# Which queue sends the first unit's stacks, and 4 passes of zeros ahead of its scores, not 18

## The chip, the core and the metric

The kernel runs on one core of a Trainium2 chip. The metric is the device time of one execution in microseconds (us), the median over the runs. A core has TensorE (PE: matmuls, with weight loads listed apart as PEld), VectorE (DVE), ScalarE (ACT), GpSimd (POOL) and SyncE (SP), and 16 DMA engines. A transfer is issued by an instruction on SP, ACT or POOL; the issuing instruction takes time on that engine's queue, and the transfer itself then runs on the DMA engines. Engines wait for each other, and for transfers, by semaphores.

## What is computed

One transformer block on x (16 batch entries of 256 tokens, 256 wide), with a conditioning vector and a context per batch entry:

```python
shift_a, scale_a, gate_a, shift_m, scale_m, gate_m = jnp.split(silu(c) @ W_mod + b_mod, 6, axis=-1)
x_norm = modulate(_ln(x), shift_a, scale_a)
q, k, v = jnp.split(x_norm @ W_qkv + b_qkv, 3, axis=-1)          # 16 heads of 16
attn_w = softmax(einsum('bhqd,bhkd->bhqk', q, k) * scale)
x = x + gate_a * (einsum('bhqk,bhkd->bhqd', attn_w, v) @ W_proj + b_proj)
...
x = x + cross_attention(_ln(x), _ln(context))
...
x = x + gate_m * (gelu(modulate(_ln(x), shift_m, scale_m) @ W_mlp1 + b_mlp1) @ W_mlp2 + b_mlp2)
```

All of it is float32. Matmuls of precision that matters are done as sums of products of a high part and a low remainder (the names with h_ or Th and l_ or Tl).

## The kernel before, in words

The work is cut into 32 units: for each batch entry one of self-attention ("s") and one of cross-attention ("c"); the MLP follows behind them. A unit needs its queries and keys in a *stack*: big[n % 3], a tile with one half for q and one for k, in which every head's rows hold the high part twice and the low part once, so that one matmul gives the precise product. A stack half is written by six transfers of 128 KB (out of h_q or h_k: words x0, x1, y0, y1; out of l_q or l_k: words l0, l1), for two column halves f = 0, 1. The function that issues one is `send` in `to_stack`; it takes the queue as an argument. Before the rows are sent, the tile is set to zero (words z0q, z0k and so on), since rows that are not sent must be zero.

The ramp, before the first unit can run, is written out by hand: the string PRE in the table E_ (line 55) lists words, and each word issues its instructions in that order. All engines keep this order in the program. The words that matter here:

- K0a, K0m: the key matmuls of unit 0 into ps_k; K0h: ScalarE reads them into h_k; K0l: VectorE makes the remainder l_k. Q0a, Q0m, Q0h, Q0l the same for queries; K1..., Q1... for unit 1.
- K0x0, K0x1, K0y0, K0y1, K0l0, K0l1 and the same with Q: the twelve sends of unit 0's stack. A word without a suffix goes on SyncE; with p, on GpSimd.
- hiv, lov: high part and remainder of V's weights (ScalarE, VectorE); V0a, V0b: the value matmuls of unit 0 (psv_s); bv: a bias product into st, added by VectorE into bqkv.
- b9: `busy(9, sp[0])`, nine matmuls of a 128 x 128 tile of zeros (wz) with itself. Each is two passes on TensorE, so the trace counts 18. Their result is not read.
- L2a, L2b, L2c: layer norm of unit 2 (VectorE's statistics, GpSimd's power and apply, xn_s), which TensorE transposes (psT_s) soon after the first scores.
- ld3: the load of x for unit 3, on SyncE.

Behind PRE, the loop over units begins with n = -1: eight beats, in which the scores of unit 0 (s_tile: q from big times k from big, into st or s) are computed and VectorE takes their row maxima (mx). These first scores are the first readers of unit 0's stack.

Transfers on the hardware queues (SP and ACT) take eight semaphores in turn, DMAHW0 to DMAHW7, and a transfer isn't issued before the one that had its semaphore last has landed. GpSimd's have semaphores of their own (DMASW).

Of the kernel before, what the change touches and what calls it, by code (L numbers as in the profile page):

```python
# [21 lines left out]
def pixart_block(  # L22
# [29 lines left out]
                return tc.keep_in_program_order(i) if self.on else i  # L52
            return issue

    E_ = {'M': (-10, -4, 1, 5), 'CUT': 8, 'LN': {'s': 'pool', 'c': 'pool', 'q': 'pool'}, 'ON': (1, 1, 1), 'L0': -16, 'L1': 1, 'S0': -7, 'A0': 0, 'T0': 1, 'S1': 5, 'A1': 7, 'L2': 9, 'T1': 9, 'S2': 32, 'AP': 23, 'DV': (0, 1), 'HP': (1, 0), 'BZ': {}, 'AV': {1: [(1, 2), (1, 3)], 9: [(0, 0), (0, 1)]}, 'AHEAD': (0, 0, 0, 0, 0, 2), 'TW': {(21, 6): 'cb', (23, 6): 'u1', (25, 1): 'u0', (25, 7): 'u2', (27, 1): 'u3', (27, 4): 'h2p', (27, 5): 'h3p', (28, 3): 'u5 h1p', (28, 4): 'h0p', (29, 0): 'l3', (29, 1): 'l0', (29, 3): 'l1d', (29, 6): 'u7', (29, 7): 'u4 u6 h4p', (30, 1): 'h5p h6d', (30, 7): 'l6', (31, 0): 'h7p', (31, 1): 'l4', (31, 2): 'l5', (31, 6): 'l7', (28, 1): 'l2'}, 'XP': 1, 'IL': 1, 'MF': 0, 'SH': 4, 'RAMP': 1, 'HA': 1, 'MP': 16, 'W': (7, 1, 0, 0), 'PRE': 'z0qp z0kp load rest ld2 one0 silu b12 brow L0a turn L0b b4 L0d scale T0t sc1 hik lok L1a T0h L1b T0l b4 shift hiq K0a L1d bk loq K0m K0h K0x0 K0x1 K0y0p K0y1p T1t K0l T1h K0l0 K0l1 bq T1l Q0a Q0m Q0h Q0x0 Q0y0p Q0x1 Q0y1p Q0l Q0l0 Q0l1 z1kp z1qp K1a K1b hiv lov Q1a Q1b K1x0 K1x1 K1y0 K1y1 K1l K1l0 K1l1 Q1x0 Q1x1 Q1y0 Q1y1 Q1l Q1l0 Q1l1 L2a L2b L2c V0a V0b bv b9 ld3', 'SL': {(-1, 0): 'V1a', (-1, 1): 'T2t T2h T2p vone z2kp z2qp', (-1, 2): 'V1b', (-1, 3): 'rest wm', (-1, 4): 'M0 rest one1 ld4', (-1, 5): 'K2a L3a', (-1, 6): 'K2m L3b L3p L3c', (-1, 7): 'mods sc2 one2 rest', (0, 0): 'gm rest', (0, 1): 'rest', (0, 4): 'rest', (0, 6): 'rest', (1, 0): 'rest', (1, 5): 'rest'}}

    PE = InOrder(nc.tensor, True)
    ACT, DVE, POOL, SP = (InOrder(e, True) for e in (nc.scalar, nc.vector, nc.gpsimd, nc.sync))
# [49 lines left out]
    brow = const.tile([32, P], F32, name="brow")  # L108
# [8 lines left out]
    def split(hi, lo, src, eng=POOL, hp=0):  # L117
        (DVE, POOL, ACT)[E_['HP'][hp]].tensor_copy(hi, src) if E_['HP'][hp] < 2 else ACT.copy(hi, src)
        eng.tensor_tensor(lo, src, hi, ALU.subtract)
# [9 lines left out]
    sc1 = const.tile([P, 2, 2, B], F32, name="sc1")  # L129
    bT = const.tile([P, 32], F32, name="bT")  # L130
    sT = const.tile([P, KC, B], F32, name="sT")
    cb = const.tile([P, H], F32, name="cb")
# [123 lines left out]
    wm = []  # L256
# [9 lines left out]
    gm = []  # L266
# [19 lines left out]
    def layernorm(src, name):  # L286
# [19 lines left out]

        def apply(eng=E_['LN'].get(name[0])):
            o.xn = work.tile([P, NT, H], F32, tag="xn", name=f"xn_{name}", bufs=3)
            if eng == "act":
                nb = work.tile([P, NT], F32, tag="nb", name=f"nb_{name}")  # L310
                DVE.scalar_tensor_tensor(nb, o.mv[:, :, 0], -1.0, o.rs, ALU.mult, ALU.mult)
            if eng not in ("act", "dve"):
                less = work.tile([P, NT], F32, tag="less", name=f"less_{name}")
                POOL.tensor_scalar(less, o.mv[:, :, 0], -1.0, None, ALU.mult)
            for t in range(NT):
                if eng == "act":
                    ACT.activation(o.xn[:, t], src()[:, t], AF.Identity, bias=nb[:, t:t + 1],
                                   scale=o.rs[:, t:t + 1])
                elif eng == "dve":
                    DVE.tensor_scalar(o.xn[:, t], src()[:, t], o.mv[:, t, 0:1], o.rs[:, t:t + 1],  # L320
                                      ALU.subtract, ALU.mult)
                else:
                    POOL.tensor_scalar(o.xn[:, t], src()[:, t], less[:, t:t + 1], o.rs[:, t:t + 1],
                                       ALU.add, ALU.mult)
# [476 lines left out]
    M = {}  # L801
# [52 lines left out]
    def mlp_T(b):  # L854
# [18 lines left out]
        for f in range(KC):  # L873
            DVE.tensor_scalar(y[:, f], pst[:, f * N:(f + 1) * N], sc1[:, 1, f, b:b + 1],
                              cpT[:, 6 + f, b:b + 1], ALU.mult, ALU.add)
        if b in E_['DV']:
            DVE.tensor_copy(hi, y)
# [111 lines left out]
    rest = setup_rest()  # L989

    u0, u1 = units[:2]
# [4 lines left out]
    u2 = units[2]  # L996
    word = {}
    for n, v in (("0", u0), ("1", u1), ("2", u2)):
        for c in "KQV":
            o = getattr(v, c)  # L1000
# [8 lines left out]
    for n, v in (("0", u0), ("1", u1), ("2", u2)):  # L1009
        word["T" + n + "t"], word["T" + n + "h"], word["T" + n + "l"] = v.T[0].parts  # L1010
        word["T" + n + "p"] = v.T[0].low_pool
        for c in "KQ":
            o = getattr(v, c)
            word[c + n + "l"] = o.parts[2]
            word[c + n + "m"], word[c + n + "h"] = o.third, o.high
            word[c + n + "p"] = o.low_pool
            for f in range(KC):
                for q, k in enumerate("xyl"):
                    word[f"{c}{n}{k}{f}"] = lambda o=o, q=q, f=f: o.send(f, q)
                    word[f"{c}{n}{k}{f}p"] = lambda o=o, q=q, f=f: o.send(f, q, POOL)  # L1020
            word[c + n + "s"] = lambda o=o: [o.send(f, q) for f in range(KC) for q in range(3)]
    for n in range(2):
        for i in range(16):
# [15 lines left out]
    u3 = units[3]  # L1039
# [9 lines left out]
    for i in range(3):  # L1049
        for n, f in (("b", f_b), ("hi", f_hi), ("lo", f_lo)):  # L1050
            word[n + "qkv"[i]] = lambda f=f, i=i: f(i)
    for w in E_['PRE'].split():
        word[w]()
    for p, ws in E_['SL'].items():
        at[p] += [word[w] for w in ws.split()]
    ACT.on, POOL.on, SP.on = E_['ON']
    at_end = defaultdict(list)
# [172 lines left out]
    last, o, q = units[-1], units[-1].post, units[-2].post  # L1230
# [115 lines left out]
```

## Time and profile before

| | before |
|---|---|
| median of 3 runs | 735.78 us (735.75 to 736.23) |
| the profiled execution | 736.51 us, of which the span 734.7 us |
| PE / DVE / ACT / POOL busy | 99% / 77% / 77% / 71% of the span |
| granted TensorE clock | 0.999 of full speed |

The span is what the trace covers; the time of the same execution is 1.8 us longer. TensorE is busy nearly all of it. The chain of waits, followed back from the end, has this share by engine:

```profile
PE 90%; POOL 2%; DVE 2%; issue 2%; ACT 2%; DMA 1%; SPq 1%; ACTq 0%; POOLq 0%; DVEq 0%
```

A row of the timeline has the start in us, the length in us, the engine, the line of the code (L51 for nearly all, where a helper records the operations), the operation, the tile written and the tiles read with their shapes, and a count when like rows are merged; in brackets, the idle time just before it and what ended it. SPq, ACTq and POOL with DMA_DIRECT2D are the issues of transfers. Rows of a table by windows have the window, its length, the busy time of PE, PEld, DVE, ACT and POOL, the granted clock, the share of the DMA engines and GB/s.

GpSimd's four issues, which the change takes from it:

```profile
13.94 1.31 POOL L51 DMA_DIRECT2D big<-h_k  x2 [1.56 <-ACT h_k L51]
16.66 1.05 POOL L51 DMA_DIRECT2D big<-h_q  x2 [1.42 <-ACT h_q L51]
```

### The profile page before, as it was taken

How to read it: one execution, taken by the hardware profiler on the slowest of the kernel's cores; microseconds unless marked ns; L12 is line 12 of the kernel's file. 1: busy time of each engine (PE TensorE's matmuls, PEld its weight loads, DVE VectorE, ACT ScalarE, POOL GpSimd, SP SyncE). 2: the span in 40 equal slices, each digit the busy share in tenths (PEclk: the TensorE clock that was granted, in tenths of full speed). 3: DMA queues.
4: the chain of work that ended last, by engine and by line, in shares of the span. 5: the costliest groups of instructions: out<-in, count | busy, mean ns of one | idle time of the engine just before them, and what ended most of it. 6: DMA issues, size and time to landing. Idle time of an engine off the chain costs nothing.

```text
span 734.7 us, 25385 instructions
## 1 busy us (share of the span) xinstructions
PE 727.2 (99%) x10092; PEld 642.2 (87%) x10092; DVE 565.7 (77%) x1164; ACT 562.8 (77%) x976; POOL 521.5 (71%) x638
## 2 busy tenths in 40 slices
PE   9999999999999999999999999999999999999997
PEld 9778888888888888888888888888889999999997
DVE  4888888988888888988888889888746765556542
ACT  4277898888888888888888888888887666666663
POOL 6757576858567575856757687888576888898873
PEclk9999999999999999999999999999999999999999
DMA  6755444543545454354545456454321644444421
GB/s 209 203 149 146 130 134 137 141 125 96 154 115 155 131 142 136 107 152 114 159 125 143 137 145 161 124 158 129 117 74 36 164 133 113 112 124 100 116 80 37
DMA packets 108906, 94.81 MB, mean 129 GB/s; under 512 B 36914, under 2 KB 92756, under 8 KB 108788
## 3 DMA queue, kind: packets, MB, share of 16 engines
q1 hardware_dynamic: 108308, 92.27, 45.5%
q8 instruction: 80, 1.31, 0.8%
q0 software_dynamic: 192, 0.52, 0.3%
q10 hardware_dynamic: 288, 0.39, 0.2%
q14 instruction: 38, 0.31, 0.1%
HBM read 30.38 MB, written 11.86 MB: 57 GB/s over the span
## 4 chain that ended last, share of the span: by engine, by line
PE 90%; POOL 2%; DVE 2%; issue 2%; ACT 2%; DMA 1%; SPq 1%; ACTq 0%; POOLq 0%; DVEq 0%
PE s L51 17%; PE o L51 16%; PE st L51 14%; PE ph L51 8%; PE ps_q L51 5%; PE ps_qc L51 5%; PE ps_kc L51 4%; PE ps_P_s L51 3%; PE ps_v_c L51 3%; PE ps_k L51 3%; PE ps_v_s L51 2%; PE ps_P_c L51 2%; PE ps_h L51 1%; PE psT_q L51 1%; PE psA_c L51 1%
## 5 line engine op out<-in xcount | busy, mean ns | idle before, releaser
L51 DVE TENSOR_REDUCE mx<-s 128x2 f32<-128x512 f32 x504 | 324.4, 683 | 64.1 <-PE s L51 57.0
L51 ACT ACTIVATE pt<-st 128x1024 f32<-128x1024 f32 x252 | 259.0, 1028 | 16.6 <-PE st L51 10.8
L51 PE MATMUL s<-big 63*128 63x256 f32 (+1 forms) x1024 | 183.5, 297 | 0.2 <-DVE mx L51 0.2
L51 PEld LDWEIGHTS s<-big 63*128 63x128 f32 (+1 forms) x1024 | 133.2, 185 | 19.0 <-DVE l_kc L51 6.6
L51 PE MATMUL st<-big 64*128 64x256 f32 (+1 forms) x1024 | 133.8, 298 | 0.3 <-ACT pt L51 0.2
L51 PE MATMUL o<-pt,v 128*32 128x256 f32 x2048 | 123.8, 382 | 0.0
L51 PEld LDWEIGHTS st<-big 64*128 64x128 f32 (+1 forms) x1024 | 95.5, 185 | 16.2 <-issue 12.9
L51 POOL TENSOR_TENSOR hl<-hf,hh 128x512 fp32r<-128x512 f32 x64 | 85.4, 1342 | 32.3 <-ACT hh L51 31.9
L51 PEld LDWEIGHTS o<-pt,v 128*32 128x32 f32 x2048 | 60.2, 109 | 41.4 <-PE psm L51 0.2
L51 ACT ACTIVATE hh<-ph,bT 128x256 fp32r<-128x256 f32 x114 | 47.9, 472 | 23.2 <-PE s L51 10.9
L51 ACT ACTIVATE hf<-ph,bT 128x256 f32<-128x256 f32 x114 | 47.6, 471 | 21.6 <-PE ph L51 21.5
L51 ACT COPY oT<-o 128x512 f32<-128x512 f32 x63 | 37.0, 587 | 33.5 <-PE o L51 33.5
L51 PE MATMUL s<-big,hh 128*128 128x256 f32 x272 | 49.8, 282 | 0.0
L51 PE MATMUL ph<-wkch,wself 128*128 128x256 f32 x224 | 44.5, 282 | 0.5 <-ACT hh L51 0.4
L51 PE MATMUL ph<-wqch,wself 128*128 128x256 f32 x224 | 44.3, 281 | 0.0
L51 PE MATMUL ps_k<-xTh_s,wself 64*128 64x256 f32 (+1 forms) x232 | 43.9, 294 | 0.0
L51 PE MATMUL st<-big,hh 128*128 128x256 f32 x240 | 43.8, 281 | 0.0
L51 DVE TENSOR_SCALAR xn_m<-x,mv_m,rs_m 128x256 f32<-128x256 f32 x28 | 28.7, 1066 | 19.1 <-POOL rs_m L51 19.1
L51 POOL CAST xTh_c<-y_c 128x512 fp32r<-128x512 f32 x16 | 9.8, 613 | 45.5 <-ACT y_c L51 45.5
L51 PEld LDWEIGHTS s<-big,hh 128*128 128x128 f32 x272 | 41.4, 188 | 0.0
L51 PE MATMUL ps_q<-xTh_s,wself 64*128 64x256 f32 (+1 forms) x240 | 39.8, 283 | 0.4 <-DVE l_q L51 0.4
L51 PE MATMUL ps_v_s<-wself,xTh_s 64*128 64x256 f32 x224 | 39.2, 294 | 0.0
(249 smaller groups left out, 2496.1 us busy)
## 6 DMA issues: line engine op xcount, KB each, us to landing
big<-h_kc SPq DMA_DIRECT2D x64, 128.0 KB
big<-h_qc SPq DMA_DIRECT2D x64, 128.0 KB
big<-h_k SPq DMA_DIRECT2D x62, 128.0 KB
big<-h_q SPq DMA_DIRECT2D x62, 128.0 KB
big<-l_k SPq DMA_DIRECT2D x32, 128.0 KB
big<-l_q SPq DMA_DIRECT2D x32, 128.0 KB
g<-gd SPq DMA_DIRECT2D x16, 256.0 KB
c<-in_ctx_dram SPq DMA_DIRECT2D x16, 256.0 KB
```

What stands on the lines that cost most here:

```text
L51: i = f(*a, **k)
```

## The change

Three words of PRE are other ones. The y sends of unit 0's keys, K0y0 and K0y1, go on SyncE instead of GpSimd; the y sends of its queries go on ScalarE instead of GpSimd (the suffix a is new); and b2 takes the place of b9, which is four passes of zeros where there were 18.

```diff
...
-K0a L1d bk loq K0m K0h K0x0 K0x1 K0y0p K0y1p T1t K0l T1h K0l0 K0l1
+K0a L1d bk loq K0m K0h K0x0 K0x1 K0y0 K0y1 T1t K0l T1h K0l0 K0l1
...
-Q0a Q0m Q0h Q0x0 Q0y0p Q0x1 Q0y1p Q0l Q0l0 Q0l1
+Q0a Q0m Q0h Q0x0 Q0y0a Q0x1 Q0y1a Q0l Q0l0 Q0l1
...
-L2a L2b L2c V0a V0b bv b9 ld3
+L2a L2b L2c V0a V0b bv b2 ld3
...
                 for q, k in enumerate("xyl"):
                     word[f"{c}{n}{k}{f}"] = lambda o=o, q=q, f=f: o.send(f, q)
                     word[f"{c}{n}{k}{f}p"] = lambda o=o, q=q, f=f: o.send(f, q, POOL)
+                    word[f"{c}{n}{k}{f}a"] = lambda o=o, q=q, f=f: o.send(f, q, ACT)
```

On SyncE, the sends of unit 0's stack (big0; h_k0, l_k0, h_q0, l_q0 are unit 0's parts) stood before like this:

```order
L51 DMA big0_75<-h_k0_241 16x8x256 [waits DMAHW2_49,Activation_49]
L51 DMA big0_75<-h_k0_241 16x8x256 [waits DMAHW3_49,Activation_49]
L51 DMA big0_75<-l_k0_253 16x8x256 [waits DMAHW4_49,DVE_49]
L51 DMA big0_75<-l_k0_253 16x8x256 [waits DMAHW5_49,DVE_49]
L51 DMA big0_75<-h_q0_282 16x8x256 [waits DMAHW6_49,Activation_49]
L51 DMA big0_75<-h_q0_282 16x8x256 [waits DMAHW7_49,Activation_49]
L51 DMA big0_75<-l_q0_289 16x8x256 [waits DMAHW0_49,DVE_49]
L51 DMA big0_75<-l_q0_289 16x8x256 [waits DMAHW1_49,DVE_49]
L51 DMA big1_76<-h_k1_309 16x8x256 [waits DMAHW2_49,Activation_49,Pool_49]
```

With the change, the same place on SyncE:

```order
L51 DMA big0_75<-h_k0_241 16x8x256 [waits DMAHW2_49,Activation_49]
L51 DMA big0_75<-h_k0_241 16x8x256 [waits DMAHW3_49,Activation_49]
L51 DMA big0_75<-h_k0_241 16x8x256 [waits DMAHW4_49]
L51 DMA big0_75<-h_k0_241 16x8x256 [waits DMAHW5_49]
L51 DMA big0_75<-l_k0_253 16x8x256 [waits DMAHW6_49,DVE_49]
L51 DMA big0_75<-l_k0_253 16x8x256 [waits DMAHW0_49,DVE_49]
L51 DMA big0_75<-h_q0_282 16x8x256 [waits DMAHW2_49,Activation_49]
L51 DMA big0_75<-h_q0_282 16x8x256 [waits DMAHW3_49,Activation_49]
L51 DMA big0_75<-l_q0_289 16x8x256 [waits DMAHW4_49,DVE_49]
L51 DMA big0_75<-l_q0_289 16x8x256 [waits DMAHW5_49,DVE_49]
L51 DMA big1_76<-h_k1_309 16x8x256 [waits DMAHW6_49,Activation_49,Pool_49]
```

Two sends stand ahead of l_k0, and the last l_q0 is the tenth of the stack on this queue, where it was the eighth.

On ScalarE, from h_q of unit 0 to h_q of unit 1, with the change (before, the two rows of DMA are not there, and GpSimd has four such rows ahead of the memset of unit 1's stack):

```order
L51 ACTIVATE h_q0_282<-ps_q0_269,bqkv_102 128x256 [waits DVE_49,PE_49]
L51 ACTIVATE h_q0_282<-ps_q0_269,bqkv_102 128x256
L51 DMA big0_75<-h_q0_282 16x8x256 [waits DMAHW7_49,Activation_49,Pool_49]
L51 DMA big0_75<-h_q0_282 16x8x256 [waits DMAHW1_49,Activation_49]
L51 ACTIVATE h_k1_309<-ps_k1_296,bqkv_102 128x256 [waits PE_49]
L51 ACTIVATE h_k1_309<-ps_k1_296,bqkv_102 128x256
L51 CAST wself_87<-wf2_114 128x512 [waits DMAHW0_49]
L51 ACTIVATE h_q1_327<-ps_q1_314,bqkv_102 128x256 [waits DMAHW4_49,DMAHW3_49,DMAHW5_49,DMAHW2_49,PE_49]
```

The h_k of unit 1, the cast of V's weights (wself out of wf2) and h_q of unit 1 now stand behind the two issues.

On TensorE, at the end of PRE, with the change:

```order
L51 MATMUL st_109<-cpT_101,wf2_114 128x16 [waits DMAHW0_49]
L51 MATMUL st_109<-cpT_101,wf2_114 128x16 x3
L51 MATMUL s0_110<-wz_66 128x128 x2
L51 MATMUL st_109<-big0_75 128x256 [waits DMAHW6_49,DMAHW4_49,DMAHW7_49,DMAHW2_49,DVE_49]
L51 MATMUL st_109<-big0_75 128x256 [waits DMAHW3_49,DMAHW5_49,DMAHW1_49,DMAHW0_49]
```

Between bv's product and the first two score matmuls stand two matmuls of zeros, where there were nine; the scores' waits are for the eight semaphores that the twelve sends now share.

More of the change, by code (lines that the diff above doesn't have):

```diff
@@ L53, in __getattr__ @@
             return issue
-    E_ = {'M': (-10, -4, 1, 5), 'CUT': 8, 'LN': {'s': 'pool', 'c': 'pool', 'q': 'pool'}, 'ON': (1, 1, 1), 'L0': -16, 'L1': 1, 'S0': -7, 'A0': 0, 'T0': 1, 'S1': 5, 'A1': 7, 'L2': 9, 'T1': 9, 'S2': 32, 'AP': 23, 'DV': (0, 1), 'HP': (1, 0), 'BZ': {}, 'AV': {1: [(1, 2), (1, 3)], 9: [(0, 0), (0, 1)]}, 'AHEAD': (0, 0, 0, 0, 0, 2), 'TW': {(21, 6): 'cb', (23, 6): 'u1', (25, 1): 'u0', (25, 7): 'u2', (27, 1): 'u3', (27, 4): 'h2p', (27, 5): 'h3p', (28, 3): 'u5 h1p', (28, 4): 'h0p', (29, 0): 'l3', (29, 1): 'l0', (29, 3): 'l1d', (29, 6): 'u7', (29, 7): 'u4 u6 h4p', (30, 1): 'h5p h6d', (30, 7): 'l6', (31, 0): 'h7p', (31, 1): 'l4', (31, 2): 'l5', (31, 6): 'l7', (28, 1): 'l2'}, 'XP': 1, 'IL': 1, 'MF': 0, 'SH': 4, 'RAMP': 1, 'HA': 1, 'MP': 16, 'W': (7, 1, 0, 0), 'PRE': 'z0qp z0kp load rest ld2 one0 silu b12 brow L0a turn L0b b4 L0d scale T0t sc1 hik lok L1a T0h L1b T0l b4 shift hiq K0a L1d bk loq K0m K0h K0x0 K0x1 K0y0p K0y1p T1t K0l T1h K0l0 K0l1 bq T1l Q0a Q0m Q0h Q0x0 Q0y0p Q0x1 Q0y1p Q0l Q0l0 Q0l1 z1kp z1qp K1a K1b hiv lov Q1a Q1b K1x0 K1x1 K1y0 K1y1 K1l K1l0 K1l1 Q1x0 Q1x1 Q1y0 Q1y1 Q1l Q1l0 Q1l1 L2a L2b L2c V0a V0b bv b9 ld3', 'SL': {(-1, 0): 'V1a', (-1, 1): 'T2t T2h T2p vone z2kp z2qp', (-1, 2): 'V1b', (-1, 3): 'rest wm', (-1, 4): 'M0 rest one1 ld4', (-1, 5): 'K2a L3a', (-1, 6): 'K2m L3b L3p L3c', (-1, 7): 'mods sc2 one2 rest', (0, 0): 'gm rest', (0, 1): 'rest', (0, 4): 'rest', (0, 6): 'rest', (1, 0): 'rest', (1, 5): 'rest'}}
@@ new lines, in pixart_block @@
+    E_ = {'M': (-10, -4, 1, 5), 'CUT': 8, 'LN': {'s': 'pool', 'c': 'pool', 'q': 'pool'}, 'ON': (1, 1, 1), 'L0': -16, 'L1': 1, 'S0': -7, 'A0': 0, 'T0': 1, 'S1': 5, 'A1': 7, 'L2': 9, 'T1': 9, 'S2': 32, 'AP': 23, 'DV': (0, 1), 'HP': (1, 0), 'BZ': {}, 'AV': {1: [(1, 2), (1, 3)], 9: [(0, 0), (0, 1)]}, 'AHEAD': (0, 0, 0, 0, 0, 2), 'TW': {(21, 6): 'cb', (23, 6): 'u1', (25, 1): 'u0', (25, 7): 'u2', (27, 1): 'u3', (27, 4): 'h2p', (27, 5): 'h3p', (28, 3): 'u5 h1p', (28, 4): 'h0p', (29, 0): 'l3', (29, 1): 'l0', (29, 3): 'l1d', (29, 6): 'u7', (29, 7): 'u4 u6 h4p', (30, 1): 'h5p h6d', (30, 7): 'l6', (31, 0): 'h7p', (31, 1): 'l4', (31, 2): 'l5', (31, 6): 'l7', (28, 1): 'l2'}, 'XP': 1, 'IL': 1, 'MF': 0, 'SH': 4, 'RAMP': 1, 'HA': 1, 'MP': 16, 'W': (7, 1, 0, 0), 'PRE': 'z0qp z0kp load rest ld2 one0 silu b12 brow L0a turn L0b b4 L0d scale T0t sc1 hik lok L1a T0h L1b T0l b4 shift hiq K0a L1d bk loq K0m K0h K0x0 K0x1 K0y0 K0y1 T1t K0l T1h K0l0 K0l1 bq T1l Q0a Q0m Q0h Q0x0 Q0y0a Q0x1 Q0y1a Q0l Q0l0 Q0l1 z1kp z1qp K1a K1b hiv lov Q1a Q1b K1x0 K1x1 K1y0 K1y1 K1l K1l0 K1l1 Q1x0 Q1x1 Q1y0 Q1y1 Q1l Q1l0 Q1l1 L2a L2b L2c V0a V0b bv b2 ld3', 'SL': {(-1, 0): 'V1a', (-1, 1): 'T2t T2h T2p vone z2kp z2qp', (-1, 2): 'V1b', (-1, 3): 'rest wm', (-1, 4): 'M0 rest one1 ld4', (-1, 5): 'K2a L3a', (-1, 6): 'K2m L3b L3p L3c', (-1, 7): 'mods sc2 one2 rest', (0, 0): 'gm rest', (0, 1): 'rest', (0, 4): 'rest', (0, 6): 'rest', (1, 0): 'rest', (1, 5): 'rest'}}
```

## Prediction

> **What bounds the kernel now.** I read the page's busy shares first, then the chain of waits, then the stages by window. TensorE is the bound nearly everywhere:
>
> ```profile
> PE 727.2 (99%) x10092; PEld 642.2 (87%) x10092; DVE 565.7 (77%) x1164; ACT 562.8 (77%) x976; POOL 521.5 (71%) x638
> 100.00:400.00 300.00, 299.93 (x4916) 254.81 (x4916) 261.12 (x561) 253.46 (x392) 205.29 (x275) 1.00 0.48 133
> ```
>
> The first row is the whole span. In the second row, 300 us of the middle, TensorE (first column after the length) is busy 299.93. So whatever shifts TensorE's start of real work shifts the end by about as much, and nothing later gives it back or adds to it, unless it makes TensorE wait. The change lies in the first 25 us, so I read the chain of waits there (start, length, what):
>
> ```profile
> 17.70 1.70 PE ps_q L51 x12
> 19.39 1.68 PE psv_s L51 x12
> 21.07 0.80 PE st L51 x8
> 21.87 2.10 PE s L51 x18
> 23.97 0.43 PE st L51 x4
> ...
> 25.74 0.59 PE psT_s L51 x4
> ```
>
> The piece of 2.10 us from 21.87 is the 18 passes of zeros; the scores follow at 23.97. The passes are on the chain, but as a cover: the first score needs all twelve stack sends of unit 0. The question is what TensorE would wait for if they went. The timeline has the first score's row without any idle time before it:
>
> ```profile
> 21.72 2.25 PE L51 MATMUL s<-wz 128*128 128x128 f32 x18
> 23.90 0.50 PE L51 MATMUL st<-big 63*128 63x256 f32 x4
> ```
>
> So at 23.90 the stacks had landed, and how long before that isn't shown. The answer must come from the queues.
>
> **The change, part by part.** *Passes.* 14 of the 18 go: 2.10 / 18 = 0.117 us each, 1.63 us. Four then end at 21.87 + 0.47 = 22.34. That is all that can be gained; it is gained only as far as the stacks are there by then.
>
> *When the stacks land.* SyncE's issues (start, length):
>
> ```profile
> 13.65 1.32 SPq L51 DMA_DIRECT2D big<-h_k  x2
> 15.07 1.30 SPq L51 DMA_DIRECT2D big<-l_k  x2
> 16.46 1.82 SPq L51 DMA_DIRECT2D big<-h_q  x2
> 18.37 1.20 SPq L51 DMA_DIRECT2D big<-l_q  x2
> 19.67 2.51 SPq L51 DMA_DIRECT2D big<-h_k  x4
> 22.28 1.20 SPq L51 DMA_DIRECT2D big<-l_k  x2
> ```
>
> Back to back, four issues go from 19.67 to 22.28: 0.65 each. Now SyncE sends unit 0's stack in ten issues, not eight, and the second l_q send is the tenth: 13.65 + 9 x 0.65 = 19.50. Before, it was issued here:
>
> ```profile
> 17.11 1.17 SPq L51 DMA_DIRECT2D big<-h_q  x1
> 19.02 0.55 SPq L51 DMA_DIRECT2D big<-l_q  x1
> ```
>
> So it goes about 0.5 later than at present. Not the full 1.3 of two more issues, because SyncE before waited in places and one issue took 1.17 rather than some 0.6; if that long one comes again, the last send goes at 20.1. How long from issue to landing? GpSimd's sends have it; for SyncE's it is bounded by two waits:
>
> ```profile
> big<-h_k POOLq DMA_DIRECT2D x1, 128.0 KB, 3.3
> big<-h_q POOLq DMA_DIRECT2D x2, 128.0 KB, 5.0
> 15.72 0.65 SPq L51 DMA_DIRECT2D big<-l_k  x1
> 20.69 0.88 DVE L51 SCALAR_TENSOR_TENSOR l_q<-ps_q,bqkv,h_q 128x256 fp32r<-128x256 f32 x2 [0.47 <-DMA big<-l_k]
> ```
>
> VectorE's l_q of unit 1 waited for the l_k sends, whose buffer it takes; the second, issued at 15.72, was there by 20.69, 4.97 later. The last l_q send was there by 23.90, at most 4.88 after 19.02. The lower end is 3.3, that of the first GpSimd send, before the engines were full. For the tenth send: 19.50 + 3.3 = 22.8, 19.50 + 4.9 = 24.4. I take the middle, 4.0 after issue, **23.5**, since the twelve sends carry the same bytes over the same DMA engines, which were full in that stretch:
>
> ```profile
> 19.00:20.00 1.00, 1.00 (x9) 0.81 (x8) 1.00 (x3) 0.40 (x2) 1.00 (x2) 1.00 1.01 223
> 20.00:21.00 1.00, 1.00 (x11) 1.00 (x10) 0.53 (x2) 0.44 (x2) 1.00 (x1) 1.00 1.13 237
> 21.00:22.00 1.00, 1.00 (x11) 1.00 (x10) 1.00 (x4) 0.59 (x1) 0.28 (x1) 1.00 1.07 245
> ```
>
> The last two columns are the DMA engines' share, 1.0 and over in the three us before the landing, and GB/s, 223 to 245. SyncE alone at 131 KB per 0.65 us asks for 202 GB/s, and ScalarE's two sends come on top. So the twelve cannot land much earlier than they do, whoever issues them. In the Trainium skill, "DMA: Bandwidth & Descriptors", section "Issuing engines are not separate DMA queues", sends from SyncE, ScalarE and GpSimd run on the same 16 DMA engines, and issuing from several saves only the issue time; by that rule the last send lands later by the 0.5 that it is issued later, and the sum stays within the bounds above. The shares of 1.0 agree with it.
>
> So the first score starts at about 23.55, where it was 23.97: **0.4 us gained**, with TensorE idle 1.2 us ahead of it. Between the ends (22.85 and 24.45) this is 1.1 gained to 0.5 lost.
>
> *ScalarE.* Its two new issues stand between h_q of unit 0 and h_k of unit 1:
>
> ```profile
> 15.89 0.84 ACT L51 ACTIVATE h_q<-ps_q,bqkv 128x256 fp32r<-128x256 f32 x2 [1.17 <-PE ps_q L51]
> 17.36 0.84 ACT L51 ACTIVATE h_k<-ps_k,bqkv 128x256 fp32r<-128x256 f32 x2 [0.63 <-PE ps_k L51]
> 18.09 0.62 ACT L51 CAST wself<-wf 128x512 fp32r<-128x512 f32 x1
> 19.60 0.84 ACT L51 ACTIVATE h_q<-ps_q,bqkv 128x256 fp32r<-128x256 f32 x2 [0.89 <-PE ps_q L51]
> 18.75 0.69 DVE L51 TENSOR_TENSOR wself<-wf,wself 128x512 fp32r<-128x512 f32 x1 [1.10 <-ACT wself L51]
> 19.49 0.19 PEld L51 LDWEIGHTS psv_s<-wself,xTh_s 128*128 128x128 f32 x1 [0.19 <-DVE wself L51]
> ```
>
> Two issues of 0.55 to 0.6 beginning near 16.5 end near 17.7 instead of the idle 0.63: h_k starts 0.3 to 0.5 late (1.0 if one is long), and behind it queue the cast of V's weights, then VectorE's remainder of them, for which TensorE's psv_s already waits 0.19. So TensorE reaches the zeros 0.4 later, at 22.3, and leaves four of them at 22.75. That is still ahead of 23.5, so it costs nothing; were the stacks early it would cost these 0.4. ScalarE's h_q of unit 1 takes the buffer of unit 0's h_k, so it waits for all four h_k sends; the last goes at 15.6 and lands near 15.6 + 4.1 = 19.7, where h_q now starts at 19.60: nothing.
>
> *VectorE and GpSimd.* VectorE's l_q of unit 1 waits for the l_k sends, now issued fifth and sixth, at 16.25 and 16.90: landing 16.90 + 4.1 = 21.0, which is 0.3 after the present 20.69 (between 20.2 and 21.9). Behind l_q stand unit 2's statistics, the add of bqkv that the first score also waits for, then GpSimd's xn_s:
>
> ```profile
> 22.36 0.16 DVE L51 TENSOR_TENSOR bqkv<-st,bT 128x32 f32<-128x32 f32 x1
> 23.89 1.10 POOL L51 TENSOR_SCALAR xn_s<-x,less_s,rs_s 128x256 f32<-128x256 f32 x2
> ```
>
> The add moves from 22.5 to 22.8, still covered; xn_s ends at 24.99 + 0.3 = 25.3, and TensorE wants it at 25.74 - 0.4 = 25.3. Just covered: nothing. GpSimd loses its four issues, and its two memsets for unit 1 move from 17.70 up to about 12.4; it is not waited for there, and they don't slow VectorE:
>
> ```profile
> 14.03 0.88 DVE L51 SCALAR_TENSOR_TENSOR l_k<-ps_k,bqkv,h_k 128x256 fp32r<-128x256 f32 x2 [1.08 <-ACT h_k L51]
> 17.70 3.58 POOL L51 MEMSET big<- 128x2048 f32 x2
> 19.35 0.87 DVE L51 SCALAR_TENSOR_TENSOR l_k<-ps_k,bqkv,h_k 128x256 fp32r<-128x256 f32 x2
> ```
>
> l_k takes 0.88 without a memset beside it and 0.87 with one. SyncE's later sends all go 0.5 later, unit 1's stack among them: at present it is issued by 27.3, and its first scores run at 36.7, a slack of over 4 us after landing.
>
> Sum: 0.4 us off, all of it from the zeros. The profiled execution took 736.51 (span 734.7), 0.73 over the median of 735.78; I put the difference on the median: 735.78 - 0.4 = **735.4**, span 734.3. 0.2% of this kernel is 1.5 us, about what a measurement tells from no change, so the forecast is "same".
>
> **Rivals.**
> *The stacks come early* (chance 0.10). GpSimd's sends took up to 5.0 to land, and without them the queue may clear sooner; if all land by 22.34, the whole 1.63 comes off: 734.15. For it: 3.3 was seen once. Against it: the DMA shares, and the tenth issue at 19.50, which would need a landing in 2.8.
>
> *Unit 2's chain is late* (0.12). The l_k sends land at 21.9, VectorE's l_q and all behind it move 1.2, xn_s ends at 26.2, and TensorE waits 0.85 for it at psT_s: 735.4 + 0.85 = 736.25. It decides from a shift of 0.3 up.
>
> *SyncE's queue is the new bound* (0.08). The long issue comes again, the last send goes at 20.1 and takes 4.9: score at 25.05, 1.1 later than now: 736.9.
>
> *The clock drops in the wait* (0.06), the slower side. TensorE starts the kernel slow:
>
> ```profile
> 1.04 5.30 PE L51 MATMUL s<-wz 128*128 128x128 f32 x24 [1.04 <-DVE wz L51]
> 729.00:731.00 2.00, 1.41 (x12) 1.20 (x11) 1.19 (x4) 0.00 (x0) 0.00 (x0) 1.00 0.00 0
> 733.00:734.00 1.00, 0.00 (x0) 0.00 (x0) 0.00 (x0) 0.00 (x0) 0.00 (x0) 0.54 0.00 0
> ```
>
> 24 passes took 5.30, where 24 x 0.117 = 2.8 is the later pace: 2.5 lost per warming. If the 1.2 us of idling brings that back at the scores: 735.4 + 2.5 = 737.9. Against it: at the end TensorE stopped near 730.4 and the granted clock (the column with 0.54) halved only about 733, some 2.6 later. The Trainium skill, "TensorE: Matmul & The Clock Gate", section "Why this matters for your kernels", asks for no gaps over about 3 us, so by it 1.2 us is safe; the end of this trace agrees.
>
> That it doesn't do what it says is part of the first rival reversed: the passes go, but the score starts at the same 23.97; this lies within the forecast's range.
>
> **How the numbers follow.** The forecast has 0.64, with its own range 734.7 to 736.3 (1.1 gained to 0.5 lost). The rivals have 0.10, 0.12, 0.08 and 0.06. Faster by over 0.2% means below 734.3: about half of the first rival, 0.05. Slower means above 737.25: the clock and a little of SyncE's case, 0.07. The rest is 0.88. The range of 734.1 to 736.9 takes in all but the clock and the tails.
>
> **What would show it.** Right: SyncE's second l_q issue near 19.5; four passes ending by 22.8; TensorE idle about 1 us, released by a DMA into big, and the first score near 23.5; ScalarE's h_k of unit 1 near 17.8; psT_s without a wait; the rest of the kernel as before. Wrong: no idling ahead of the score (stacks early), an idle psT_s released by GpSimd, SyncE's issue after 20, a granted clock below 1.0 behind the wait, or a difference that arises after 40 us.

## The result, and the profile after

| | before | after |
|---|---|---|
| median of 7 runs each, same chip | 736.23 us (735.75 to 740.30) | 740.85 us (740.22 to 742.77) |
| the profiled execution (span) | 736.51 us (734.7) | 740.22 us (738.4) |
| mean granted clock of that execution | 0.999 | 0.995 |

The ratio is 1.0061, with a 95% interval of 1.0040 to 1.0082: slower by 4.6 us, outside the range on record, 734.1 to 736.9. One of all executions here and below was slow, with 1349.81 us: one of the ten of the run half, and it is left out of the ratio.

The page of after, busy shares:

```profile
PE 728.0 (99%) x10078; PEld 642.3 (87%) x10078; DVE 571.3 (77%) x1164; ACT 561.8 (76%) x976; POOL 518.9 (70%) x634
```

14 passes are gone, and TensorE is busy 0.8 us longer. To find where, I compared the chains of waits of the first 30 us. After (start, length, what):

```profile
11.33 4.84 DVE xn_s L51
...
16.22 1.22 PE psT_s L51 x4
17.44 1.52 PE st L51 x8
18.96 2.76 PE ps_q L51 x12
...
21.75 0.48 ACT h_q L51
...
25.88 1.58 PE psv_s L51 x11
...
28.25 0.54 PE s L51 x4
28.79 0.43 PE st L51 x3
```

The same stretch of the chain before:

```profile
13.11 0.44 PE psT_s L51 x4
13.55 0.80 PE st L51 x8
14.35 1.52 PE ps_q L51 x12
...
15.89 0.85 ACT h_q L51 x2
```

Laid beside each other, the two chains account for the first score step by step. psT_s, the transposes of unit 1's xn_s, starts 16.22 - 13.11 = **3.1 us late**. Then the same three groups take 1.22 + 1.52 + 2.76 = 5.50 instead of 0.44 + 0.80 + 1.52 = 2.76: **2.7 more**. From there to the zeros the lag grows from 21.75 - 15.89 = 5.86 to 28.25 - 21.87 = 6.38: **0.5 more**. Four passes of zeros take 0.54 instead of 2.10: **1.6 less**. The first score is at 28.79 instead of 23.97, 4.8 late. That is the loss at the first score. It stays for a long while: the first scores of unit 1 run at 41.77 instead of 36.73, 5.0 late. The two profiled executions end only 3.7 us apart (738.4 and 734.7), so 1.3 are regained later; 0.41 of it is a wait of TensorE before, at 617.85, that it doesn't have after, and the rest is not traced. The medians are 4.6 apart.

What stood in front of psT_s? The timeline of after, rows of GpSimd, VectorE and TensorE (start, length, engine):

```profile
11.27 1.27 POOL L51 TENSOR_TENSOR wself<-wf,wself 128x512 fp32r<-128x512 f32 x1
12.47 3.55 POOL L51 MEMSET big<- 128x2048 f32 x2
11.33 5.15 DVE L51 TENSOR_SCALAR xn_s<-x,mv_s,rs_s 128x256 f32<-128x256 f32 x2 [0.26 <-POOL rs_s L51]
16.22 1.22 PE L51 MATMUL psT_s<-ident,xn_s 128*128 128x128 f32 x4 [3.09 <-DVE xn_s L51]
28.72 0.50 PE L51 MATMUL st<-big 63*128 63x256 f32 x4
```

GpSimd's two memsets for unit 1's stack (words z1kp, z1qp) follow its remainder of the weights (loq) at once. VectorE's two xn_s take 5.15 us together, and TensorE sits idle 3.09 us for them. Before, the same two engines looked like this; the memsets came at 17.70, behind GpSimd's four issues:

```profile
11.11 1.27 POOL L51 TENSOR_TENSOR wself<-wf,wself 128x512 fp32r<-128x512 f32 x1
11.18 1.68 DVE L51 TENSOR_SCALAR xn_s<-x,mv_s,rs_s 128x256 f32<-128x256 f32 x2 [0.19 <-POOL rs_s L51]
```

The view of the tile xn_s gives shortest, median and longest of the two in ns. After, then before:

```profile
L51 DVE TENSOR_SCALAR xn_s<-x,mv_s,rs_s x2: 395/2613/4831, 11.3 to 16.1; 128x256 f32<-128x256 f32 x2
```

```profile
L51 DVE TENSOR_SCALAR xn_s<-x,mv_s,rs_s x2: 401/878/1354, 11.2 to 12.4; 128x256 f32<-128x256 f32 x2
```

One xn_s runs alone in 0.40 us in both. The other begins 0.06 or 0.07 us after GpSimd's remainder, and does not end until GpSimd is done with what it has in a row: 1.35 us before, when that was the remainder alone, 4.83 us after, when two memsets followed it. In the Trainium skill, "SBUF — State Buffer", section "Who interferes with whom", VectorE and GpSimd share a pair of SBUF ports as an exclusive lock: a tensor_scalar in a mode that takes both ports and a GpSimd instruction block each other for their whole length. The 4.83 beside 0.40 agrees, though no run here shows which mode this tensor_scalar ran in; that the waiting instruction is passed over for three GpSimd instructions in a row is this trace's.

The 2.7 us is the clock. Windows of after (start to end, length, busy PE, PEld, DVE, ACT, POOL, granted clock, DMA share, GB/s):

```profile
14.00:15.00 1.00, 0.00 (x0) 0.00 (x0) 1.00 (x1) 0.00 (x0) 1.00 (x2) 0.89 0.00 0
15.00:21.00 6.00, 4.78 (x22) 4.65 (x23) 3.43 (x8) 1.64 (x4) 1.02 (x1) 0.50 0.27 71
21.00:22.00 1.00, 1.00 (x8) 1.00 (x7) 0.00 (x0) 0.25 (x1) 0.00 (x0) 0.69 0.81 217
```

0.89 and 0.69 in the outer windows put the halved stretch at about 14.8 to 21.6, 6.8 us. TensorE had been idle since 13.1, so it fell 1.7 us into the wait, and it stayed down for 5.4 us of work: at half speed a loss of 2.7.

### The profile page after: what moved, and what is told of

Read it like the earlier page. It is cut to its first block, busy times and chain, and to the rows that moved or that the text cites. A ratio compares the mean times of both kernels' runs of the same rounds, so it can differ in the third digit from the quotient of the medians.

```text
span 738.4 us, 25351 instructions
## 1 busy us (share of the span) xinstructions
PE 728.0 (99%) x10078; PEld 642.3 (87%) x10078; DVE 571.3 (77%) x1164; ACT 561.8 (76%) x976; POOL 518.9 (70%) x634
## 4 chain that ended last, share of the span: by engine, by line
PE 94%; DVE 2%; ACT 1%; issue 1%; DMA 1%; POOL 1%; SPq 0%; ACTq 0%; POOLq 0%; DVEq 0%
PE s L51 17%; PE o L51 16%; PE st L51 15%; PE ph L51 11%; PE ps_qc L51 5%; PE ps_q L51 4%; PE ps_kc L51 3%; PE ps_P_s L51 3%; PE ps_v_s L51 3%; PE ps_v_c L51 3%; PE ps_k L51 2%; PE ps_P_c L51 2%; PE ps_h L51 1%; PE psT_q L51 1%; PE psA_s L51 1%
## 5 line engine op out<-in xcount | busy, mean ns | idle before, releaser
L51 POOL TENSOR_TENSOR hl<-hf,hh 128x512 fp32r<-128x512 f32 x64 | 86.2, 1354 | 32.4 <-ACT hh L51 32.3
L51 ACT ACTIVATE hf<-ph,bT 128x256 f32<-128x256 f32 x114 | 47.6, 470 | 19.8 <-PE ph L51 19.7
```

Of the source, the lines that this page charges most:

```text
L51: i = f(*a, **k)
```

## The experiments

The theories: **the memsets** (they block VectorE's xn_s, psT_s waits, the clock falls, all else follows) against **the queues** (the sends on SyncE and ScalarE are what is late) and **the passes** (without the 18 passes the clock falls ahead of the scores). Each run was compared with the kernel before on the same chip; "score" is the first matmul that reads unit 0's stack, at 23.90 before and 28.72 after. In the order E_ the word "..." stands for unchanged words.

**gate.** After, with one tiny GpSimd copy ahead of the two memsets, that reads h_q of unit 0, so that they come as late as they did before. It needs a new tile of 8 bytes per partition.

```diff
+    gate_t = const.tile([P, 2], F32, name="gate_t")
...
+    word["gp"] = lambda: POOL.tensor_copy(gate_t, u0.Q.hi[:, 0, 0:2].bitcast(F32))
...
-Q0l Q0l0 Q0l1 z1kp z1qp K1a
+Q0l Q0l0 Q0l1 gp z1kp z1qp K1a
```

> The changed kernel, with one small copy on GpSimd (two elements of unit 0's h_q) put ahead of the two memsets of unit 1's stack, so that they cannot start before about 16.8 us, as before the change. Theory P (the memsets, no longer held back by GpSimd's issues, keep VectorE's xn_s of unit 1 waiting): xn_s takes 1.7 us for the pair, not 5.2, TensorE has no stall at psT_s, the clock stays at 1.0, and the first score comes at 23.5 as predicted, so 735.2 to 736.0, ratio 0.999 to 1.000. Theory Q (the sends' new queues are what costs): still 740 to 741, ratio about 1.006.

Measured: 734.97 us (10 runs), ratio 0.9975 (0.9960 to 0.9990). The two xn_s take 403 and 1350 ns, as before. The memsets and scores in the timeline:

```profile
16.52 3.56 POOL L51 MEMSET big<- 128x2048 f32 x2
23.64 0.68 PE L51 MATMUL st<-big 63*128 63x256 f32 x4 [0.56 <-DVE bqkv L51]
```

With the queues and the zeros of after, and the memsets back at 16.52, the stall is gone and so is the whole loss. So the loss needs the early memsets. The score waits 0.56 for VectorE's add into bqkv, which ends at 23.6 here; the prediction had it at 22.8 and covered. That it came out faster than before was not yet explained (see gate_same_tile and pad).

**early_zero.** The counterpart: the kernel before, all its sends and its 18 passes as they were; only the memsets go ahead of GpSimd's issues.

```diff
-bk loq K0m K0h K0x0
+bk loq K0m z1kp z1qp K0h K0x0
...
-Q0l Q0l0 Q0l1 z1kp z1qp K1a
+Q0l Q0l0 Q0l1 K1a
```

> The kernel before, all four sends still on GpSimd and 18 passes, but with the two memsets of unit 1's stack ahead of GpSimd's issues. Theory P: xn_s is held as in the changed kernel, and with 18 passes the first score comes about 1.6 later than there, or later still since GpSimd's sends of h_k go only after 16 us: 741 to 744, ratio 1.007 to 1.011. Theory Q: no send has changed its queue, so 736, ratio 1.000.

Measured: 742.03 us (4 runs), ratio 1.0074 (1.0055 to 1.0094). The two xn_s take 4837 and 395 ns. Timeline:

```profile
12.37 3.55 POOL L51 MEMSET big<- 128x2048 f32 x2
16.12 1.22 PE L51 MATMUL psT_s<-ident,xn_s 128*128 128x128 f32 x4 [3.09 <-DVE xn_s L51]
30.03 0.50 PE L51 MATMUL st<-big 63*128 63x256 f32 x4
```

No send has changed its queue, and the same 4.84, the same 3.09 and a halved clock (0.50 from 16 to 22 us) are there. GpSimd's own sends are later here too, as they stand behind the memsets, but the score waits for none of them. Together with gate, this shows the memsets' place as the cause, and the queues of the sends as no direct part of it but the 0.5 above.

**passes_only.** The kernel before with b2: the zeros alone.

```diff
-bv b9 ld3
+bv b2 ld3
```

> The kernel before with 4 passes of zeros, sends as before. By my prediction's sum and theory P: the first score waits for the last l_q send, which lands by 23.9, so it starts between 23.0 and 23.9 and the time is 735.3 to 736.2, ratio 0.999 to 1.000; TensorE idles 0.7 to 1.5 us at full clock. Theory Z (the missing zeros cost, by the clock): the clock drops after 22.3 and the time is 738 to 741.

Measured: 736.83 us (10 runs), ratio 1.0005 (0.9988 to 1.0022): no difference. Timeline and windows:

```profile
23.73 0.82 PE L51 MATMUL st<-big 63*128 63x256 f32 x4 [1.18 <-DMA big<-h_k]
```

```profile
24.00:25.00 1.00, 1.00 (x7) 0.81 (x7) 0.41 (x1) 0.00 (x0) 0.90 (x4) 0.82 0.66 192
25.00:28.00 3.00, 3.00 (x15) 2.22 (x16) 2.02 (x3) 0.16 (x1) 0.48 (x1) 0.50 0.77 209
28.00:29.00 1.00, 1.00 (x9) 0.87 (x10) 0.67 (x2) 1.00 (x4) 0.00 (x0) 0.98 0.57 159
```

The score comes 0.2 earlier than before, behind 1.18 us of idling, and then the clock halves for 3.4 us of full work, a loss of 0.18 + 1.50 + 0.02 = 1.7. So the passes alone gain next to nothing, and this execution (737.94) lost more. The median lies between the ranges of the two theories; Z's drop of the clock is there in the trace, a loss of Z's size in the median is not. "TensorE: Matmul & The Clock Gate" in the Trainium skill, section "Why this matters for your kernels", warns of gaps over about 3 us. In after the clock fell 1.7 us into a gap of 3.09, and here 0.9 behind the end of one of 1.18, both sooner than that, so the measurement decides. That the gap of 1.18 is what lowered the clock is not shown.

**queues_b9.** After, with the 18 passes back: the queues alone.

```diff
-bv b2 ld3
+bv b9 ld3
```

> The changed kernel with the 18 passes back. Theory P: the stall ahead of psT_s stays, and since no wait stands ahead of the first score in the changed kernel, the 14 passes add their whole 1.6 us: 742 to 743, ratio 1.008 to 1.009. Theory Z: as before, 736. Theory Q: 740 to 741 with a first score where the changed kernel has it.

Measured: 741.71 us (4 runs), ratio 1.0067 (1.0049 to 1.0085). Timeline:

```profile
29.56 0.50 PE L51 MATMUL st<-big 63*128 63x256 f32 x4
```

The 14 passes cost 0.9 us in the medians (741.71 against 740.85, of two sessions, with overlapping intervals), not the full 1.63. The stacks were there, since the score follows without a wait; but by the trace xn_s stalled TensorE for 2.5 here and not 3.1, and the clock halved once more at 41.6. Of the change's two parts, the queue part carries the loss.

**gate_same_tile.** gate was faster than before, which the memsets don't explain. Here the copy writes a tile that exists already, so that no address moves.

```diff
+    word["gp"] = lambda: POOL.tensor_copy(dummy, u0.Q.hi[:, 0, 0:2].bitcast(F32))
```

> The same gate as in the run gate, but its small copy writes an existing tile (dummy), so that no tile moves to another address. If the gate itself explains that run's 735.0 (1.2 below before), this takes 735.0 again, ratio 0.9975. If 8 bytes more per partition in front of later tiles made TensorE's matmuls faster there (the rows by window show 174 matmuls in 20 us late in the kernel, before 172), this one has 172 and takes 735.6 to 736.2, ratio 0.999 to 1.000, and the predicted 0.4 is all that the change with the gate brings.

Measured: 736.55 us (10 runs), ratio 1.0010 (0.9998 to 1.0023). Score at 23.17, 0.7 earlier than before. The loss is gone without the tile too, but the time is not below before. Most of the 0.7 is gone by the second scores into st, at 26.09 instead of 26.25, since psT_s waits for unit 2's xn_s (see unit 2's chain in the part on the prediction). Then the clock costs more: the runs have a median clock of 0.9975 where the kernel before has 0.999, some 0.0015 x 735 = 1.1 us, and in the profiled execution it halves from 37.3 to 40.7.

**pad.** The kernel before with the unused 8 bytes alone.

```diff
+    gate_t = const.tile([P, 2], F32, name="gate_t")
+    POOL.memset(gate_t, 0.0)
```

> The kernel before, with a tile of 8 bytes per partition added at the place where the run gate has its own, set to zero at the start and read by nothing. If the address of later tiles matters: faster by 1 to 2 us, ratio 0.997 to 0.999, and 174 matmuls in 20 us late in the kernel. If not: 736.2, ratio 1.000, and 172.

Measured: 735.24 us (10 runs), ratio 0.9984 (0.9975 to 0.9993). A window late in the kernel and one group of matmuls (count, busy, mean ns), before and then pad:

```profile
580.00:600.00 20.00, 20.00 (x172) 20.00 (x171) 13.29 (x18) 13.56 (x33) 17.47 (x16) 1.00 0.51 129
L51 PE MATMUL s<-big,hh 128*128 128x256 f32 x272 | 49.8, 282 | 0.0
```

```profile
580.00:600.00 20.00, 20.00 (x174) 20.00 (x173) 13.86 (x20) 13.49 (x32) 18.16 (x16) 1.00 0.47 122
L51 PE MATMUL s<-big,hh 128*128 128x256 f32 x272 | 48.4, 278 | 0.0
```

The same matmuls run 1.4% faster, 174 instead of 172 in 20 us. gate has the 174 too, gate_same_tile the 172. So a good part of gate's lead over before is this, and no effect of the gate.

**half.** After, with the keys' two y sends back on GpSimd, ahead of the memsets; the queries' stay on ScalarE, and the zeros are four.

```diff
-K0x0 K0x1 K0y0 K0y1 T1t
+K0x0 K0x1 K0y0p K0y1p T1t
```

> The changed kernel with the y sends of unit 0's keys back on GpSimd, those of its queries still on ScalarE, 4 passes. Theory P: GpSimd's two issues wait for h_k until 13.9 and stand ahead of the memsets, which then run from 15.3; VectorE's xn_s is done by 12.9, no stall, first score near 23.5: 735.2 to 736.5, ratio 0.999 to 1.000 (up to 1.002 where the clock drops for a window). Theory Q: half of the loss of 4.6 us or more stays: 738 to 741.

Measured: 735.50 us (10 runs; the ratio is of nine), ratio 0.9984 (0.9973 to 0.9996). Timeline:

```profile
14.96 3.58 POOL L51 MEMSET big<- 128x2048 f32 x2
22.83 0.69 PE L51 MATMUL s<-wz 128*128 128x128 f32 x4
23.45 0.50 PE L51 MATMUL st<-big 63*128 63x256 f32 x4
```

Two issues are enough to hold the memsets behind xn_s (0.40 and 1.35 again), with nothing added to the program.

**warm.** To part the stall from the clock: after, with 28 passes of zeros put ahead of the transposes, where TensorE waits. They shorten no wait.

```diff
-K0x0 K0x1 K0y0 K0y1 T1t
+K0x0 K0x1 K0y0 K0y1 b14 T1t
```

> The changed kernel with 28 more passes of zeros on TensorE ahead of psT_s of unit 1 (28 x 0.117 = 3.3 us, about as long as the stall there), so that TensorE is busy while it would wait. The stall stays: VectorE's xn_s still ends near 16.5. Theory P with the clock as its second part: the clock stays at 1.0 past 14.8, the work from 16.2 to 21.6 takes half as long, and the time is 2 to 3.4 us less than the changed kernel's 740.85: 737.5 to 738.8, ratio 1.002 to 1.0035. If the clock had no part: 740.9, ratio 1.006.

Measured: 739.05 us (5 runs), ratio 1.0033 (1.0018 to 1.0047). The zeros and the score in the timeline, and a window from the end of the stall on:

```profile
12.96 3.29 PE L51 MATMUL s<-wz 128*128 128x128 f32 x28
26.11 0.51 PE L51 MATMUL st<-big 63*128 63x256 f32 x4
```

```profile
16.00:22.00 6.00, 5.56 (x47) 5.22 (x46) 2.94 (x9) 3.26 (x9) 0.00 (x0) 1.00 0.51 141
```

xn_s takes 4.84 as in after, but the clock stays at 1.00, and the score comes at 26.11 instead of 28.72. So the clock's share is 2.6 at the score, as the chain says (0.1 of it because psT_s starts at 16.08 here, in after at 16.22), and 1.8 in the medians (739.05, a little over the range expected); the stall's remains. The two ratios' intervals overlap, so it is the trace that settles it, and not the times.

**norm_stt.** The other way to avoid the block: the memsets stay early, and unit 1's xn_s is done by another instruction of VectorE.

```diff
+                 elif eng == "stt":
+                     DVE.scalar_tensor_tensor(o.xn[:, t], src()[:, t], o.mv[:, t, 0:1],
+                                              o.rs[:, t:t + 1].to_broadcast([P, H]), ALU.subtract, ALU.mult)
...
-K0a L1d bk
+K0a L1t bk
```

> The changed kernel (memsets on GpSimd from 12.5 us), with VectorE's xn_s of unit 1 computed by another instruction: scalar_tensor_tensor with the reciprocal deviation as a broadcast operand, in place of tensor_scalar. If it is this form of instruction that is held by GpSimd's memsets (VectorE's l_k, a scalar_tensor_tensor, takes 0.88 with or without a memset beside it), the pair ends by 13.4 at the latest, after GpSimd's remainder of the weights at 12.5, psT_s waits 0.5 us or less, the clock stays: 735.5 to 737, ratio 0.999 to 1.001. If any VectorE instruction that reads SBUF is held: xn_s ends at 16.5 again and 740 to 741, ratio 1.006.

Measured: 736.49 us (10 runs), ratio 1.0001 (0.9989 to 1.0013). Tile view and timeline:

```profile
L51 DVE SCALAR_TENSOR_TENSOR xn_s<-x,mv_s,rs_s x2: 474/978/1482, 11.2 to 12.6; 128x256 f32<-128x256 f32 x2
```

```profile
12.37 3.56 POOL L51 MEMSET big<- 128x2048 f32 x2
```

The memsets run at 12.37, as early as in after, and VectorE ends its second xn_s at 13.1 beside them; psT_s follows at 13.13 without a wait. The first one took 1.48 and ended with GpSimd's remainder of the weights, which reads SBUF. So it is not the memset as such that blocks VectorE, but the memset against this form of instruction.

**half_k.** half the other way round: the keys' y sends on SyncE as in after, the queries' on GpSimd.

```diff
-Q0x0 Q0y0a Q0x1 Q0y1a
+Q0x0 Q0y0p Q0x1 Q0y1p
```

> The changed kernel with the y sends of unit 0's queries back on GpSimd, those of its keys on SyncE, 4 passes. Theory P: GpSimd waits for h_q until 16.7, the memsets run from 17.7, no stall at psT_s: 735.2 to 736.5, ratio 0.999 to 1.000. Theory Q, in the form that two more issues on SyncE cost: 737 or more, ratio 1.001 to 1.006.

Measured: 737.16 us (10 runs), ratio 1.0007 (0.9990 to 1.0024). Timeline:

```profile
19.11 1.21 SPq L51 DMA_DIRECT2D big<-l_q  x2
21.75 0.69 PE L51 MATMUL s<-wz 128*128 128x128 f32 x4
22.84 0.83 PE L51 MATMUL st<-big 63*128 63x256 f32 x4 [0.41 <-DMA big<-l_q]
```

The first score is 1.1 us earlier than before, the best of the kernels without the 8 bytes, and in the profiled execution the span is 733.4. But the ten runs go from 734.91 to 739.95, with granted clocks from 1.000 down to 0.992, the longest at the lowest. The median lies in theory Q's range, but the interval reaches into both, and the trace shows no loss ahead of the score: the gain there is seen, and a lower clock in other executions goes with its loss. What lowers the clock is not shown.

**half_pad.** half and pad's two lines together.

```diff
-K0x0 K0x1 K0y0 K0y1 T1t
+K0x0 K0x1 K0y0p K0y1p T1t
...
+    gate_t = const.tile([P, 2], F32, name="gate_t")
+    POOL.memset(gate_t, 0.0)
```

> The kernel of the run half (735.5 there) with the tile of 8 bytes of the run pad (1.1 off there). If the two add up, as one acts ahead of the first scores and the other on the pace of matmuls late in the kernel: 734.2 to 734.8, ratio 0.997 to 0.998, faster than both kernels. If they don't: 735.2 to 735.6.

Measured: 733.23 us (5 runs, 731.90 to 733.78), ratio 0.9954 (0.9940 to 0.9967): 3.4 us faster than before. half and pad are worth 0.16% each when alone, so the sum would be 0.32%; the interval of the pair lies a little beyond it. Its score is at 22.65, 0.8 ahead of half's. In the two profiled executions ScalarE's two issues make this difference: from 16.19 they take 2.24 in half, from 16.32 they take 1.33 here, and the zeros start at 22.83 and at 22.03. Whether half's other executions have the long issue is not known, so why the pair gains more than the sum is not settled.

## Why the prediction was wrong

*The step that failed* is in the part on VectorE and GpSimd: "GpSimd loses its four issues, and its two memsets for unit 1 move from 17.70 up to about 12.4; it is not waited for there, and they don't slow VectorE". The move was right to 0.1 us (12.47). The conclusion was drawn from the rows of l_k, 0.88 without a memset and 0.87 beside one. But l_k is the instruction beside the memsets at their old place, a scalar_tensor_tensor that reads PSUM. At the new place stands xn_s, a tensor_scalar from SBUF to SBUF, and its row was not looked at. The warning was in the trace before: two like xn_s of 401 and 1354 ns, the long one beside GpSimd's remainder. It was priced at nothing and cost 3.1 us of stall; gate, early_zero and norm_stt show it from three sides. The stall brought the halved clock with it, another 2.7 at the first score.

*The clock* was a rival with a chance of 0.06, 2.5 us, placed at the scores. Its price was right, 2.7 at the first score by the chain and 2.6 by warm (1.8 in the medians). Its place was not: it fell in the stall at psT_s. At the scores of after there was no wait at all. The argument against it, that the clock had halved only some 2.6 us after TensorE stopped at the end of the trace, doesn't hold as a rule: it fell 1.7 us into the stall, and in passes_only within a microsecond of the end of an idle time of 1.18.

*The landing* was put at 23.5, 4.0 behind an issue of the last l_q send at 19.50. It can't be read in after, where everything came late. The other runs have two l_q issues each, the second some 0.65 behind the first. In half_k, with the keys' sends on SyncE as in after, the first starts at 19.11, so the second near 19.8, and the score waits for l_q until 22.84, 3.1 behind the issue. In gate_same_tile, with all the sends of after, they start at 20.11, and the scores run at 23.17 without a wait for a send, 2.4 behind the second. In norm_stt they start at 20.60, and later matmuls of the score wait for l_q until 23.86, 2.6 behind the second. In passes_only, with the sends of before, the second goes near 19.0, and the score waits for a send until 23.73, up to 4.7 behind it. So the time of landing was about right, at most 0.4 to one side and 0.7 to the other, but not for the reason given: in gate_same_tile and norm_stt, which have all the sends of after, the last issue came 1.3 to 1.8 later than 19.50, and the landing 1.4 to 1.6 sooner behind it than 4.0. The two errors cancelled, which is luck. In these four runs the landing doesn't lie a fixed time behind the issue: the issues lie 2.3 us apart, the landings 1.0.

*The zeros* went for 2.10 - 0.54 = 1.56, as forecast; in after the whole of it was gained, since the stall gave the stacks time to land.

*ScalarE's two issues* were to start h_k of unit 1 0.3 to 0.5 late (1.0 if one is long), and to cost 0.4 only "were the stacks early". This is the 0.5 that the chain of after loses between h_q and the zeros: in after h_k starts at 23.75, 2.0 behind h_q, before at 17.36, 1.5 behind it, and between them stand the two issues, 1.41 from 22.30. Where the memsets were put right it can be read off the zeros: they start at 21.75 in half_k, which has no sends on ScalarE, and at 22.83 in half, which has them, one of them 1.5 long (at 22.40 in gate_same_tile and 22.03 in half_pad, which have no long one). So this term was right in kind, 0.3 to 1.1 in size, and in half on the path, because in half the stacks had landed by the end of the zeros.

*SyncE's queue and unit 2's chain*, the two other rivals, were not what cost time in after: the scores don't wait for a send there. With the stall away they show. The chain of waits of gate_same_tile (start, length, what):

```profile
18.09 3.11 DMA big<-l_k
...
24.46 1.10 POOL xn_s L51 x2
...
25.61 0.55 PE psT_s L51 x3
```

SyncE's second l_k send goes at 18.09, where the prediction had 16.90, since the issue ahead of it is long (the pair takes 2.15, before 1.30). VectorE's l_q of unit 1 waits for it until 21.28 (predicted 21.0), and behind it xn_s of unit 2 ends at 25.56 (predicted 25.3, "just covered"). psT_s waits for it. The scores ahead of psT_s come 0.55 earlier than before, those behind it 0.16: unit 2's chain costs 0.4, half of the rival's 0.85, and the prediction's own sum had it at nothing. In time gate_same_tile is the same as before within the interval, which is the forecast's class and 1.1 us from its number.

What stays open: when the clock falls in kernels without a long idle time, and what part of the differences under 0.3% is the clock's. The runs of one kernel differ by 2 to 6 us, most of the longer ones at the lower clocks, and none of these runs controls it.

## What to carry to other kernels

Taking an instruction off an in-order queue moves everything behind it forward: look up what will stand beside each of those instructions in its new place, on the engine that shares a resource with it, and not what stood beside it in the old one. A pair of like rows of which one is three times the other (0.40 and 1.35) can be a collision already present, as it was here, and hints at what a longer neighbour will cost. A wait that an instruction seemed to pay for nothing can be the thing that keeps two engines apart; when it goes, put the order back on purpose (here two sends left on GpSimd).

## What was not expected of the hardware

VectorE's tensor_scalar was held through three GpSimd instructions in a row, 4.83 us for 0.40 of work, having begun 0.06 us after the first of them. A scalar_tensor_tensor of the same size ran beside the same memsets (norm_stt, 0.47).

8 bytes more per partition ahead of the other tiles, not used by anything, change the pace of matmuls hundreds of microseconds later from 282 to 278 ns, and the kernel by 0.16% (0.07 to 0.25). In three pairs that differ by this tile (before and pad, gate_same_tile and gate, half and half_pad) the faster one is the one that has it. That it is the tiles' addresses, and which tile's, was not tried.

The granted clock also halves where TensorE had no wait of a microsecond: in queues_b9 it fell at 41.6, and TensorE was busy in all of the 5 us from 36 to 41. Windows of gate, whose TensorE was busy all but 0.23 of the two microseconds ahead:

```profile
34.00:36.00 2.00, 1.77 (x17) 1.54 (x16) 2.00 (x5) 0.71 (x2) 1.14 (x3) 1.00 0.17 49
36.00:37.00 1.00, 1.00 (x7) 0.61 (x7) 0.77 (x3) 0.00 (x0) 0.90 (x3) 0.83 0.47 117
37.00:40.00 3.00, 3.00 (x15) 1.45 (x14) 1.73 (x4) 0.46 (x2) 2.55 (x4) 0.50 0.16 54
```

It is back at 0.97 from 40 to 41, so the halved stretch has the 3.4 us that it has in passes_only, half of after's 6.8. In the clock records of all 13 traces, which the windows average, every stretch at one clock between two changes is a whole multiple of 3.41 us long. The first rise comes at 4.0 to 6.6 us after the first instruction, so the same place in the kernel meets these steps at another point in each execution; whether that is why runs of one kernel differ is not shown.
